# Two-part attention kernel: normalising the second part's sums by a ScalarE copy and a GpSimd product

## Chip, cores and metric

The kernel runs on one core of one Trainium2 chip. Times are device microseconds of one execution. The engines are named as the profile has them: PE is TensorE (PEld its weight loads), DVE is VectorE, ACT is ScalarE, POOL is GpSimd, SP issues the DMAs.

## What is computed

The input is x, of shape (8, 512, 128). The first part adds a causal attention with 16 heads of width 8, whose weights come from four Newton steps. The second part applies six layers, each with a local attention (16 heads of width 64, windows of 32 positions that also see the window before) and a feed-forward block. The place that is changed belongs to the local attention. Cut to that:

```
for i in range(6):
    x = attn_layer(shift_tokens(x), Wqkv[i], q_scale[i], k_scale[i], Wo[i]) + x
    x = ffn_layer(shift_tokens(x), ln_g[i], ln_b[i], W1[i], b1[i], W2[i], b2[i]) + x

# in attn_layer, after l2 norm and rotary embedding of q and k
sim  = einsum('bhwie,bhwje->bhwij', bq, bk2) * 8.0      # 32 queries, 64 keys a window
attn = softmax(where(mask, -max, sim), -1)
out  = einsum('bhwij,bhwje->bhwie', attn, bv2)          # the sums of v
return out.reshape(...) @ Wo
```

The softmax's division is done last: exponentials are not normalised, v carries a column of ones, and the sums of v are divided by the sum that this column gives.

## The kernel before

The first part is a generator (`stieltjes`) that is advanced a few steps at a time by the second part's loop. It runs alone at first, then beside the second part, and is used up about 3600 us into the span; from there on the second part runs alone.

The second part goes through 48 units (a sequence and a layer). A unit has eight pairs of heads, and a pair is one turn of the main loop, so there are 384 turns. Quarters of a unit hold two pairs. One turn does work for several pairs at once:

- `turn` transposes the queries and keys of the newest pair (L629, PE) and copies them out of PSUM (L634, ACT, tiles qT);
- `gather` takes the pair that is three turns older: 64 small matmuls (L683) put its sums of v, and the sums of the exponentials, into a PSUM tile named po2 (po in the profile, which leaves numbers out); L691 takes the reciprocals and L692 the product, both on DVE, into the SBUF tile o2;
- `turn_weights` transposes the exponentials of the pair between (L672) and copies them out (L673, ACT, tile prT);
- `prepare_qk` projects q and k for a later quarter: L563 (PE, tile m), square on ACT (L569), sums of squares on DVE (L572), product with the rotary tables on DVE (L573), sum of halves on POOL (L580), then L586 on DVE, L587 and L588 on ACT for the norms, and the product with them on POOL (L591);
- `exponentials` runs L665 on ACT;
- `turn_sums` transposes o2 (L700, PE) and copies it out (L704, ACT);
- `weigh` computes the scores (L648, PE), adds the band (L653, DVE), takes the maximum (L658, DVE) and subtracts it (L659, POOL);
- `prepare_v` projects v (L600, PE; L603, ACT), and `spread` sends it through DMA into its layout by windows;
- `leave` multiplies by the output weights (L708, PE). A unit ends with an add to xT, and a feed-forward block (L729 to L781) is spread over the turns that follow.

The PSUM tile of the scores and that of the sums of v share one buffer: tag "two" in a pool with one buffer of two banks. L648 can therefore start only when the sums have left it.

The order of instructions on each engine is made when the kernel is built, by a scheduler that works from the program's dependences; on the chip each engine takes its own queue in order. Only a few places are held by hand, through `follow` on ACT. An instruction that waits therefore holds all that is queued behind it on its engine.

Of the kernel before, what the change touches and what calls it, by code (L numbers as in the profile page):

```python
# [12 lines left out]
ALU = mybir.AluOpType  # L13
# [3 lines left out]
P = 128  # L17
N = 512
NT = N // P
# [10 lines left out]
DHL = 64  # L30
# [20 lines left out]
def tile_kernel(  # L51
# [18 lines left out]
    nc = tc.nc  # L70
# [604 lines left out]
    def gather(a):  # L675
        g, p, prT = a["g"], a["p"], a["prT"]
        po = ps_b.tile([P, 2, N], F32, name="po2", tag="two")
        po = po[:, :, 0 : NT * (DHL + 1)].rearrange("p e (c f) -> p e c f", c=NT)
        for n in range(NQ):
            c, u = n // UB, n % UB  # L680
            for e in range(2):
                rows = slice(e * KB, (e + 1) * KB)
                nc.tensor.matmul(  # L683
                    po[u * QB : (u + 1) * QB, e, c, :],
                    lhsT=prT[rows, c, u * QB : (u + 1) * QB],
                    rhs=g["v3"][rows, n, p, :],
                    start=True, stop=True,
                )
        a["o"] = o = tp.tile([P, NT, 2, DHL], F32, name="o2", bufs=2)
        rs = tp.tile([P, 2, NT], F32, name="rs", bufs=2)  # L690
        nc.vector.reciprocal(rs, po[:, :, :, DHL])  # L691
        nc.vector.tensor_tensor(  # L692
            o.rearrange("p c e f -> p e c f"), po[:, :, :, 0:DHL],
            rs.unsqueeze(3).to_broadcast([P, 2, NT, DHL]), ALU.mult,
        )

    def turn_sums(a):
# [136 lines left out]
    while t < slots + LAG + 1 or parts:  # L834
        i, p = t // PQ, t % PQ
# [10 lines left out]
        if last:  # L846
            gather(last)
# [103 lines left out]
```

## Time and profile before

| | |
|---|---|
| median of 3 runs | 5065.17 us (5059.89 to 5066.66) |
| the profiled execution | 5068.51 us, span 5066.8 us |
| mean granted TensorE clock | 0.932 |
| busy | PE 83%, DVE 82%, ACT 69%, POOL 59% |
| L691 (reciprocals), DVE | 384 instructions, 198 ns each |
| L692 (product), DVE | 384 instructions, 685 ns each |

The profile is one execution; shares are of its span. A group's line gives the source line, engine and operation, what is written and read, the count, the busy time and the mean of one, and then the idle time of the engine just before these instructions with what ended most of it. In the lines by stretch the columns are the stretch, its length, then busy time and count of PE, PEld, DVE, ACT and POOL, the granted clock, the DMA share and GB/s. In a timeline the columns are start, length, engine, line, operation, and in brackets the idle time before.

### The profile page before, as it was taken

The numbers are of one execution on the slowest core, as the hardware profiler recorded it, in microseconds if no ns is written. First come the engines' busy times: TensorE is split into PE (matmuls) and PEld (weight loads), VectorE is DVE, ScalarE is ACT, GpSimd is POOL, SyncE is SP. The second block draws the span as 40 slices with busy tenths as digits, with TensorE's granted clock in tenths as the row PEclk, the third lists the DMA queues.
The fourth block names the chain that finished last, engine by engine and source line by source line (L and its number), as shares of the span: only waits on it lengthen the run. The fifth ranks groups of instructions, "written<-read, shape, count | busy, mean of one in ns | idle before, by whom it ended". The sixth has DMA issues, their size and how long they took to land. (4 is left out here: it accounts for less than half of the span.)

```text
span 5066.8 us, 166956 instructions
## 1 busy us (share of the span) xinstructions
PE 4207.6 (83%) x68749; PEld 2541.9 (50%) x68749; DVE 4134.0 (82%) x9460; ACT 3515.5 (69%) x6298; POOL 2980.1 (59%) x3821
## 2 busy tenths in 40 slices
PE   4556598888888887798888888888999999989998
PEld 1223254555555554455555555455655555555554
DVE  6678688988888998888898999888777777777775
ACT  6777677777777777767777877778555555555554
POOL 3345366656666565665666666566566666666663
PEclk6667699999999998899999999999999999999999
DMA  2000022222222221222222222122333232332322
GB/s 66 1 24 18 11 65 51 58 69 51 62 55 64 63 53 35 53 64 53 57 53 63 49 52 63 42 63 56 83 73 75 67 82 66 75 78 68 81 65 54
DMA packets 558921, 288.95 MB, mean 57 GB/s; under 512 B 97580, under 2 KB 541264, under 8 KB 558160
## 3 DMA queue, kind: packets, MB, share of 16 engines
q1 hardware_dynamic: 558160, 278.26, 22.8%
q8 instruction: 543, 8.90, 0.8%
q14 instruction: 218, 1.79, 0.1%
HBM read 66.21 MB, written 7.34 MB: 15 GB/s over the span
## 5 line engine op out<-in xcount | busy, mean ns | idle before, releaser
L580 POOL TENSOR_TENSOR qn<-qr 128x512 f32<-128x512 f32 x768 | 978.0, 1278 | 1374.5 <-DVE qr L573 920.9
L573 DVE TENSOR_TENSOR qr<-m,tab 128x1024 f32<-128x1024 f32 x768 | 928.1, 1216 | 29.3 <-POOL qn L591 1.7
L563 PE MATMUL m<-wqkv,xs 128*128 128x512 f32 x1536 | 772.1, 619 | 63.6 <-ACT qT L634 42.5
L591 POOL TENSOR_TENSOR qn<-qn,ss 128x512 f32<-128x512 f32 x768 | 785.7, 1045 | 59.6 <-ACT ss L588 57.7
L572 DVE TENSOR_REDUCE ss<-qr 128x8 f32<-128x512 f32 x768 | 515.4, 677 | 291.5 <-ACT qr L569 290.1
L281 ACT ACTIVATE d<-ns,lam 128x416 f32<-128x416 f32 (+7 forms) x1024 | 574.3, 623 | 197.1 <-DVE lam L299 159.9
L634 ACT COPY qT<-ptq 128x512 f32<-128x512 f32 x768 | 424.7, 583 | 312.4 <-PE ptq L629 311.2
L264 POOL TENSOR_TENSOR df<-ns,lam 128x160 f32<-128x160 f32 (+7 forms) x1024 | 398.8, 427 | 393.2 <-DVE lam L299 337.3
L569 ACT ACTIVATE qr<-m 128x512 f32<-128x512 f32 x768 | 455.3, 599 | 208.4 <-PE m L563 203.2
L284 DVE BATCH_NORM_STATS2 stw<-d 128x6 f32<-128x416 f32 (+7 forms) x1024 | 518.3, 561 | 96.8 <-ACT d L282 95.7
L600 PE MATMUL pv<-wqkv,xs 128*128 128x256 f32 x1536 | 447.9, 414 | 166.2 <-ACT oT L704 105.1
L629 PEld LDWEIGHTS ptq<-ident,qn 128*128 128x128 f32 x3072 | 362.7, 143 | 243.7 <-issue 136.0
L629 PE MATMUL ptq<-ident,qn 128*128 128x128 f32 x3072 | 444.7, 280 | 32.3 <-DVE qr L573 18.1
L603 ACT COPY v<-pv 128x512 f32<-128x512 f32 x384 | 225.1, 586 | 310.9 <-PE pv L600 193.1
L252 PE MATMUL s<-kn,qj 32*32 32x416 f32 (+15 forms) x4096 | 375.0, 446 | 72.7 <-DVE mn L256 62.3
L659 POOL TENSOR_TENSOR pr<-pr,nm 128x512 f32<-128x512 f32 x384 | 401.2, 1045 | 40.7 <-DVE nm L658 36.0
L316 PE MATMUL dTp<-ident,ns 128*128 128x128 f32 x1280 | 253.6, 310 | 189.9 <-POOL ns L264 84.3
L708 PE MATMUL acc<-oT,wo 128*128 128x512 f32 x768 | 398.8, 601 | 3.8 <-ACT oT L704 3.8
L683 PE MATMUL po<-v,prT 64*32 64x65 f32 x24576 | 391.9, 226 | 11.7 <-DVE pr L653 9.7
L563 PEld LDWEIGHTS m<-wqkv,xs 128*128 128x128 f32 x1536 | 264.5, 196 | 260.4 <-issue 133.8
L600 PEld LDWEIGHTS pv<-wqkv,xs 128*128 128x128 f32 x1536 | 266.3, 194 | 254.2 <-ACT oT L704 149.0
L282 ACT ACTIVATE d<-d 128x1856 f32<-128x1856 f32 (+1 forms) x256 | 392.4, 1533 | 0.0
(135 smaller groups left out, 8139.0 us busy)
## 6 DMA issues: line engine op xcount, KB each, us to landing
v<-v SPq DMA_DIRECT2D x2304, 65.0 KB
v<-v SPq DMA_DIRECT2D x768, 48.8 KB
wqkv<-in_L_ffn_Wqkv_dram SPq DMA_DIRECT2D x72, 256.0 KB
v<-v SPq DMA_DIRECT2D x384, 32.5 KB
wqkv<-in_L_ffn_Wqkv_dram SPq DMA_DIRECT2D x72, 128.0 KB
wo<-in_L_ffn_Wo_dram SPq DMA_DIRECT2D x36, 256.0 KB
tab<-tabs SPq DMA_DIRECT2D x36, 256.0 KB
w<-in_L_ffn_W_dram SPq DMA_DIRECT2D x18, 341.0 KB
```

Source lines behind the costliest of these rows:

```text
L281: nc.scalar.activation(o, n, AF.Ln, bias=lam[:, c : c + 1])
L284: nc.vector.bn_stats(t["st"][:, 4 * rb + a].rearrange("p u k -> p (u k)"), o)
L563: nc.tensor.matmul(m.rearrange("p t h e -> p t (h e)"), lhsT=xs[:, c * P : (c + 1) * P], rhs=wqkv[:, 0:2, q0 : q0 + HQ * DHL], start=True, ...
L569: marks["act"] = nc.scalar.activation(sq, m.rearrange("p t h e -> p (t h) e"), AF.Square)
L572: nc.vector.tensor_reduce(ss[:, i, :], sq, axis=AX.X, op=ALU.add)
L573: nc.vector.tensor_tensor(qr, m.unsqueeze(1).to_broadcast([P, 2, 2, HQ, DHL]), tab[:, i].rearrange("p (k t) e -> p k t e", k=2).unsqueeze( ...
L580: nc.gpsimd.tensor_tensor(g["qn"][:, c].rearrange("p t h (u e) -> p (t h) u e", u=2), halves_of[:, 0], halves_of[:, 1, :, ::-1, :], ALU.add,)
L591: nc.gpsimd.tensor_tensor(qc, qc, ss[:, i, :].unsqueeze(2).to_broadcast([P, 2 * HQ, DHL]), ALU.mult)
L600: nc.tensor.matmul(pv[:, i], lhsT=xs[:, c * P : (c + 1) * P], rhs=cols, start=True, stop=True,)
L629: nc.tensor.transpose(pt[:, c * P : (c + 1) * P], g["qn"][:, c, t, 2 * p : 2 * p + 2, :].rearrange("p h e -> p (h e)"), ident,)
L634: nc.scalar.copy(q, pt)
L659: nc.gpsimd.tensor_tensor(flat, flat, nm.unsqueeze(2).to_broadcast([P, 2 * NT, KB]), ALU.add)
```

## The change

After the gather, the sums of v are copied from PSUM to o2 by ScalarE as they are; VectorE takes the reciprocals; GpSimd multiplies o2 by them in place. One line more stands in the file, so later lines count one up: the copy is L692, the reciprocals L693, the product L694, and the transposes of `turn_sums` L701.

```
         a["o"] = o = tp.tile([P, NT, 2, DHL], F32, name="o2", bufs=2)
         rs = tp.tile([P, 2, NT], F32, name="rs", bufs=2)
+        oe = o.rearrange("p c e f -> p e c f")
+        nc.scalar.copy(oe, po[:, :, :, 0:DHL])
         nc.vector.reciprocal(rs, po[:, :, :, DHL])
-        nc.vector.tensor_tensor(
-            o.rearrange("p c e f -> p e c f"), po[:, :, :, 0:DHL],
-            rs.unsqueeze(3).to_broadcast([P, 2, NT, DHL]), ALU.mult,
+        nc.gpsimd.tensor_tensor(
+            oe, oe, rs.unsqueeze(3).to_broadcast([P, 2, NT, DHL]), ALU.mult,
         )
```

The built program's order is made anew with these instructions, on all engines.

## The prediction

> **What bounds the kernel now.** I read the page first, then the groups, then busy time by stretch, then the timeline of one turn of the main loop. The page shows five engines of which none is busy throughout; the two GpSimd rows are the price list for the new multiply, a 128x512 product with one broadcast operand.
>
> ```profile
> span 5066.8 us, 166956 instructions
> PE 4207.6 (83%) x68749; PEld 2541.9 (50%) x68749; DVE 4134.0 (82%) x9460; ACT 3515.5 (69%) x6298; POOL 2980.1 (59%) x3821
> L591 POOL TENSOR_TENSOR qn<-qn,ss 128x512 f32<-128x512 f32 x768 | 785.7, 1045 | 59.6 <-ACT ss L588 57.7
> L659 POOL TENSOR_TENSOR pr<-pr,nm 128x512 f32<-128x512 f32 x384 | 401.2, 1045 | 40.7 <-DVE nm L658 36.0
> ```
>
> The groups give what goes away (L692), what a ScalarE copy out of PSUM costs (L673), and who waits for the old product (L700).
>
> ```profile
> L692 DVE TENSOR_TENSOR o<-po,rs 128x512 f32<-128x512 f32 x384 | 262.9, 685 | 7.0
> L700 PE MATMUL po<-ident,o 128*128 128x128 f32 x1536 | 243.0, 280 | 98.8 <-DVE o L692 62.9 <-ACT prT L673 16.7 <-DVE sw L294 6.9
> L673 ACT COPY prT<-pT 128x512 f32<-128x512 f32 x384 | 225.1, 586 | 184.6 <-PE pT L672 184.0
> ```
>
> The stretches show that the average over the span hides two regimes: from 600 to 3500 us both parts run together and VectorE is the busiest; from 3600 us the second part runs alone and TensorE is, at 91%, with VectorE at 74%.
>
> ```profile
> 600.00:3500.00 2900.00, 2483.95 (x40055) 1479.52 (x40048) 2558.24 (x6084) 2195.47 (x3898) 1790.49 (x2368) 0.95 0.23 56
> 3600.00:5000.00 1400.00, 1272.10 (x23423) 822.71 (x23417) 1033.72 (x1726) 808.80 (x1624) 870.97 (x853) 1.00 0.31 74
> ```
>
> L691 runs once per turn of the loop, and the same view filtered by L691 counts 216 turns in the first stretch (13.43 us a turn) and 155 from 3600 us on. The timeline of one late turn has the whole question in it: what GpSimd is doing while the sums wait to be transposed.
>
> ```profile
> 4265.31 1.28 POOL L580 TENSOR_TENSOR qn<-qr 128x512 f32<-128x512 f32 x1 [1.04 <-DVE ss L586]
> ...
> 4265.90 0.96 PE L683 MATMUL po<-v,prT 64*32 64x65 f32 x64
> ...
> 4266.54 2.05 POOL L591 TENSOR_TENSOR qn<-qn,ss 128x512 f32<-128x512 f32 x2
> ...
> 4266.90 0.21 DVE L691 RECIPROCAL rs<-po 128x8 f32<-128x8 f32 x1 [1.07 <-PE po L683]
> 4267.15 0.69 DVE L692 TENSOR_TENSOR o<-po,rs 128x512 f32<-128x512 f32 x1
> ...
> 4267.28 1.88 PE L563 MATMUL m<-wqkv,xs 128*128 128x512 f32 x4
> 4267.48 0.59 ACT L673 COPY prT<-pT 128x512 f32<-128x512 f32 x1 [0.79 <-PE pT L672]
> ...
> 4268.54 1.05 POOL L659 TENSOR_TENSOR pr<-pr,nm 128x512 f32<-128x512 f32 x1
> ```
>
> L700 follows at 4269.00 without a wait: L672 and L563 on TensorE cover the 0.9 us that VectorE needs. TensorE runs from one instruction to the next, so here the product costs nothing.
>
> **Part by part.** *Taken from VectorE:* 384 x 0.685 = 263 us. After 3600 us this frees nothing: VectorE next waits 1.20 us for the square (L569), which comes from L563. In the middle it takes VectorE from 2558/216 = 11.84 us a turn to 11.15, below TensorE's 2484/216 = 11.50.
>
> *Put on ScalarE:* 384 copies at 0.586 = 225 us. The order of the built program puts the copy between the last qT copy (L634) and prT (L673). ScalarE waits there anyway: 0.79 us in the turn shown, 184.0 us over 182 turns. The copy would run from 4266.90 to 4267.49, just where prT starts. I put it at nothing on the late path; without that cover it delays prT by up to 0.59 us, and prT is wanted a turn later. In the middle ScalarE goes from 10.16 to 10.75 us a turn, still not the busiest. The PSUM pair of banks is released by the copy's end, 0.35 us before the old product's, long before L648 needs it.
>
> *Put on GpSimd:* 384 products, nearest rows L591 and L659 (one operand broadcast over 64, 1045 ns); the upper end is L580 (1278 ns, two full operands). I take 1.045.
>
> *The new wait.* L694 stands in GpSimd's queue behind whatever is there. In the built order, of the last 114 turns 109 have both L591s and L659 ahead of it and the next L580 behind; TensorE still issues L701 right after L672 and the two L563, as before. So in the turn shown: GpSimd is free at 4269.59, L694 ends at 4270.63, L701 starts 0.14 later (the delay between L692 and L700 where TensorE does wait, at 4252.36 and 4252.50): 4270.77 against 4269.00. TensorE stands for 1.8 us, and L648, L600, the output product and the next turn's L563 queue behind it; ScalarE's oT (L704) and the v copy wait for those.
>
> Does GpSimd's chain shift along? It starts from L563 of the turn before, ahead of that turn's stall in TensorE's queue, so most of a first stall doesn't push the next; only L648's result, through L653 ahead of the second L573 on VectorE, does, and L653 has 1.2 us of slack (scores end 4262.15, L653 starts 4263.35). One unit, eight turns from 3700 us, has these shortfalls if nothing else moved (GpSimd free + 1.04 + 0.14, less the start of L700): 1.87, 2.49, 0.35, 1.98, 1.87, and three below zero, where feed-forward matmuls lengthen the turn. With each stall carried on, and the chain late by the larger of the shift two turns back and the last shift less 1.2: 1.9, then 2.49 + 0.67 - 1.87 = 1.3, 0, 2.0, 0.7, 0, 0, 0. Sum 5.8 us a unit. 152 turns from 3623 us are 19 units: **+110 us**. Lower end, by the loop that cannot be escaped (L700 to L648 to L653 to L573 to L580, two L591, L659, L694, L701: 1.44 + 0.60 + 1.36 + 1.23 + 2.0 + 1.0 + 1.04 + 0.14 = 8.8 us against turns of 8.28, 8.01, 8.05, 8.14 and 8.52): 3.0 a unit, +58. With 1278 ns for L694 the same steps give 6.7 a unit, +128.
>
> The Trainium skill speaks against this change in "GPSIMD Engine Reference", section "Engine selection": elementwise work on two inputs belongs on VectorE, and GpSimd takes about twice as long. The rows here say 1045 against 685, a factor of 1.5; by the rule's two, L694 would take 1.37 us and the late stretch would cost some 136 us, an estimate from that page.
>
> *The middle.* Gain: if the turn follows its busiest engine, from VectorE's 11.84 to TensorE's 11.50, 13.43 x 0.34/11.84 = 0.39 a turn, 83 us; at most the whole 0.69, 149 us. Loss: L694 behind GpSimd's queue, the shortfall worked out as above, is 0.87 a turn on average, 188 us if all of it stood. But TensorE idles 13.43 - 11.50 = 1.9 us a turn and its order is looser. I pass on a third, 63 us, nearer to little than to all: L700 waited there for L692 29.7 us in all, though VectorE was the fullest. Net **-20**, between -149 and +188.
>
> *The shared memory side.* Rows first: L742, a VectorE tensor_scalar on 128x128, took 1.13 us at 4249.63 beside a GpSimd L591 that ended at 4250.68, and 0.30 each at 4252.28 with GpSimd idle; L586 averages 253 ns against a median of 165. GpSimd's share rises by 401/5067 = 8 points, and 384 x 0.088 us of L586's excess at 59% makes 34 us, so 5 us more: **+5**.
>
> "GPSIMD Engine Reference", section "Key points", says more: GpSimd shares its SBUF interfaces with VectorE, and contends also with VectorE instructions that have two SBUF inputs. It gives no price, and no row here isolates such an instruction.
>
> **The sum.** 5068.5 (the profiled execution, span 5066.8 and 1.7 around it) + 110 - 20 + 5 = 5163.5. The median of the runs lies 3.3 below the profiled one: 5160.
>
> **The rivals.** *The middle pays for the late stretch (faster), 0.09.* VectorE is the fullest there at 88%; if the whole 0.685 x 216 = 149 us comes through and the late stretch costs its lower 58, the time is 5065 - 91 = 4974. It decides once the middle gains more than 110/216 = 0.51 us a turn. Against it: TensorE, at 11.50 us, is hardly less full, and waits more.
>
> *The late wait is covered (slightly faster), 0.06.* If L591 and L659 came earlier than the trace has them, only the middle's -20 is left: 5045. Against it: their inputs come from L573 and L588, which follow L563 of the same turn.
>
> *The middle stalls too, 0.09.* If the 0.87 a turn is passed on in full and VectorE's relief is lost, 5065 + 110 + 188 = 5363. For it: in the middle L264 stands in GpSimd's queue in runs of 8 or 16, and a run of 16 took 9.78 us at 3018.98, waiting on lam; 20 turns of the built order have 8 of them just ahead of L694. Against it: TensorE's idle time.
>
> **How the numbers follow.** The forecast has 0.76. Its own bounds, lower late cost with the balanced middle gain and upper late cost with a lost gain, are 5065 + 58 - 83 = 5040 and 5065 + 128 + 63 = 5256; I give 5040 to 5255, which leaves out the first and third rivals, 0.18 in all. A measurement of this kernel tells about 0.2% (10 us) from no change. Faster 0.13 (0.09 from the first rival, 0.04 from the second), same 0.05 (0.02 from the second, 0.03 from the forecast's low end), slower 0.82 (0.73 from the forecast, 0.09 from the third rival).
>
> **What would show it.** Right: from 3600 us on, TensorE idle before L701 with L694 as releaser, about 5.8 us a unit, units of 81 us instead of 75; GpSimd busy from L580 to L694 without a gap; VectorE's share down by 5 points; L694 near 1045 ns; ScalarE's wait before prT shorter by about the copy. The middle should be within some tens of us of its length. Wrong: L701 starting without a wait in late turns (the cover holds), L694 far from 1.0 us, or a middle that gets shorter by more than 110 us.

## The result, and the profile after

The changed kernel takes 5329.47 us (median of 4 runs, 5320.59 to 5335.71) against 5065.91 us before (4 runs, 5059.89 to 5071.55): a ratio of 1.0519, 95% interval 1.0498 to 1.054. It is slower, by 263.6 us; forecast were 95 us, and the range ended at 5255. One execution of the experiments below (dve_product_rf, 7832 us beside 5151 to 5164) was in a slower state and is left out of its median. The profiled execution took 5320.59 us, at a mean granted clock of 0.915 (before: 0.932).

The page after, the two lines that answer to those shown first in the prediction:

```profile
span 5318.9 us, 167209 instructions
PE 4296.5 (81%) x68749; PEld 2583.3 (49%) x68749; DVE 3967.9 (75%) x9076; ACT 3729.3 (70%) x6682; POOL 3371.4 (63%) x4205
```

VectorE is relieved, and TensorE, with exactly the same 68749 matmuls, is busy for 89 us more than before: its matmuls have become longer on average. The groups after, with the new product (L694), the transposes (L701), prT (L673), the new copy (L692) and the reciprocals (L693):

```profile
L694 POOL TENSOR_TENSOR o<-o,rs 128x512 f32<-128x512 f32 x384 | 400.3, 1043 | 316.7 <-DVE rs L693 260.4 <-DVE sw L294 28.5 <-DVE lam L299 9.6
...
L701 PE MATMUL po<-ident,o 128*128 128x128 f32 x1536 | 273.1, 303 | 382.0 <-POOL o L694 374.8 <-ACT prT L673 3.6 <-ACT pr L665 1.8
...
L673 ACT COPY prT<-pT 128x512 f32<-128x512 f32 x384 | 227.6, 593 | 19.0 <-PE pT L672 18.3
L692 ACT COPY o<-po 128x512 f32<-128x512 f32 x384 | 225.5, 587 | 77.4 <-PE po L683 76.5 <-issue 0.2
...
L693 DVE RECIPROCAL rs<-po 128x8 f32<-128x8 f32 x384 | 76.7, 200 | 325.1 <-ACT o L692 324.7
```

Before, TensorE stood 98.8 us ahead of the transposes; now 382.0, nearly all for L694. The product's own length is what the neighbouring rows said (1043 ns). And VectorE's reciprocals, which read only PSUM, wait 324.7 us for ScalarE's copy of the same tile.

To compare the same work, I cut each profile at the starts of the reciprocals, one to a turn, 384 in all:

| us | to turn 16 | turns 16 to 232 (both parts) | turns 232 to 383 (second part alone) |
|---|---|---|---|
| before | 787 | 2844 | 1406 |
| after | 807 | 2953 | 1529 |
| difference | +20 | +109 | +123 |

What is behind the last turn is 30 us in both. Busy time by stretch, cut at turns 16, 232, 240 and 376, so that before and after hold the same work (the second line is 17 units of the late stretch). Before:

```profile
787.20:3631.07 2843.87, 2449.68 (x39687) 1462.21 (x39687) 2501.07 (x5888) 2138.62 (x3802) 1753.00 (x2295) 0.96 0.24 56
3706.31:4985.16 1278.85, 1160.57 (x21400) 750.11 (x21399) 941.09 (x1567) 736.99 (x1480) 797.72 (x780) 1.00 0.31 73
```

After:

```profile
806.99:3760.15 2953.16, 2482.67 (x39672) 1483.26 (x39672) 2425.49 (x5668) 2244.18 (x4010) 1972.75 (x2510) 0.94 0.23 54
3841.47:5227.11 1385.64, 1211.16 (x21399) 770.06 (x21398) 858.27 (x1430) 821.36 (x1617) 934.40 (x916) 0.96 0.29 67
```

Late, a unit went from 1278.85/17 = 75.2 us to 81.5. Of these 6.3 us, TensorE's idle time is 3.3 (118.28 to 174.48 over 17 units) and its busy time 3.0 (1160.57 to 1211.16), with the granted clock down from 1.00 to 0.96. In the middle the 109 us are 76 of idle time and 33 of longer matmuls.

The timeline of one late turn after the change, with other rows left out, shows the wait as the prediction had it: copy, reciprocals, and then GpSimd's queue.

```profile
4199.76 1.27 POOL L580 TENSOR_TENSOR qn<-qr 128x512 f32<-128x512 f32 x1 [1.32 <-DVE ss L586]
...
4200.99 2.04 POOL L591 TENSOR_TENSOR qn<-qn,ss 128x512 f32<-128x512 f32 x2
...
4201.74 0.58 ACT L692 COPY o<-po 128x512 f32<-128x512 f32 x1 [0.20 <-PE po L683]
...
4202.35 0.21 DVE L693 RECIPROCAL rs<-po 128x8 f32<-128x8 f32 x1 [2.07 <-ACT o L692]
...
4202.99 1.04 POOL L659 TENSOR_TENSOR pr<-pr,nm 128x512 f32<-128x512 f32 x1
...
4203.99 1.04 POOL L694 TENSOR_TENSOR o<-o,rs 128x512 f32<-128x512 f32 x1
...
4205.08 0.66 PE L701 MATMUL po<-ident,o 128*128 128x128 f32 x4 [1.12 <-POOL o L694]
```

Copy and reciprocals are done at 4202.56; GpSimd needs until 4205.03, because L591 twice and L659 are ahead. The turn before started its L701 at 4196.19, 8.89 us earlier.

What the prediction had no term for is seen on TensorE's own timeline (TensorE alone) around one longer wait of the late stretch:

```profile
4412.37 1.12 PE L701 MATMUL po<-ident,o 128*128 128x128 f32 x4 [2.86 <-POOL o L694]
4413.41 1.18 PE L648 MATMUL s<-qT,qT 64*32 64x64 f32 x64
4414.53 2.07 PE L600 MATMUL pv<-wqkv,xs 128*128 128x256 f32 x4
4416.39 1.91 PE L709 MATMUL acc<-oT,wo 128*128 128x512 f32 x2
...
4423.51 0.66 PE L701 MATMUL po<-ident,o 128*128 128x128 f32 x4 [0.67 <-POOL o L694]
4424.10 0.86 PE L648 MATMUL s<-qT,qT 64*32 64x64 f32 x64
4424.89 1.13 PE L600 MATMUL pv<-wqkv,xs 128*128 128x256 f32 x4
```

The same L701 takes 1.12 us after a wait of 2.86 and 0.66 after one of 0.67; L648 1.18 against 0.86, L600 2.07 against 1.13. The stretches over this place give the granted clock (the third column from the right):

```profile
4412.40:4414.50 2.10, 2.10 (x68) 1.63 (x68) 0.00 (x0) 0.58 (x1) 1.14 (x1) 0.50 0.09 22
4414.50:4416.50 2.00, 2.00 (x11) 1.62 (x6) 1.86 (x4) 0.00 (x0) 0.00 (x0) 0.50 0.00 0
4416.50:4420.00 3.50, 3.50 (x46) 1.94 (x45) 0.63 (x2) 1.02 (x3) 2.27 (x2) 0.70 0.00 0
```

TensorE stands 2.86 us, and then runs at half clock for some 6 us: the mean of 0.70 in the last stretch is half clock up to about 4418.6 and full clock after it. Such a wait (2.8 to 3.0 us) comes once in most late units, for instance at 4330.64, 4412.37 and 4494.48, 82 us apart.

In the middle the wait is longer and rarer. One turn from the timeline of all engines:

```profile
2038.34 0.58 ACT L692 COPY o<-po 128x512 f32<-128x512 f32 x1 [1.61 <-PE po L683]
...
2043.68 7.58 POOL L264 TENSOR_TENSOR ns<-ns,lam 128x416 f32<-128x416 f32 x10 [1.62 <-DVE lam L299]
...
2047.51 0.20 DVE L693 RECIPROCAL rs<-po 128x8 f32<-128x8 f32 x1
...
2051.22 3.10 POOL L264 TENSOR_TENSOR df<-ns,lam 128x160 f32<-128x160 f32 x8
...
2054.28 2.23 POOL L264 TENSOR_TENSOR ns<-ns,lam 128x224 f32<-128x224 f32 x6
...
2056.47 1.04 POOL L694 TENSOR_TENSOR o<-o,rs 128x512 f32<-128x512 f32 x1
...
2057.57 1.11 PE L701 MATMUL po<-ident,o 128*128 128x128 f32 x4 [8.95 <-POOL o L694]
```

The reciprocals wait in VectorE's queue, 8.59 us beyond the copy's end at 2038.92, and are done at 2047.71. Then the first part's 24 L264 stand ahead of L694 in GpSimd's queue, so it runs 8.76 us later, and TensorE stands 8.95 us. Over the whole middle, TensorE's waits after the change:

```profile
PE po L701 <- POOL o L694: 199.8, 126, 8.9
```

(Total us, times, longest.) Before, the same stretch (600 to 3600 us) had 31.1 us of waits of L700 for L692.

How much later the sums are ready can be read turn by turn from the traces. From the last matmul of a gather (L683) to the end of the instruction that the transposes wait for, mean us a turn:

| | turns 16 to 232 | turns 232 to 383 |
|---|---|---|
| before | 3.22 | 1.37 |
| after | 5.32 | 3.45 |
| of what is added: the copy | 0.59 | 0.59 |
| the reciprocals' wait after the copy | 1.01 | 0.26 |
| the product's wait after the reciprocals, in VectorE's queue before and GpSimd's after | 0.16 (0.63 to 0.79) | 1.00 (0.15 to 1.15) |
| the longer product | 0.36 | 0.35 |

The rest is the wait ahead of the first of these instructions, which hardly changed. So late it is mostly GpSimd's queue; in the middle the new step on ScalarE, and VectorE's queue behind it, are the larger part.

### The profile page after: what moved, and what is told of

Read it like the earlier page. It is cut to its first block, busy times and chain, and to the rows that moved or that the text cites. A ratio compares the mean times of both kernels' runs of the same rounds, so it can differ in the third digit from the quotient of the medians.

```text
span 5318.9 us, 167209 instructions
## 1 busy us (share of the span) xinstructions
PE 4296.5 (81%) x68749; PEld 2583.3 (49%) x68749; DVE 3967.9 (75%) x9076; ACT 3729.3 (70%) x6682; POOL 3371.4 (63%) x4205
## 5 line engine op out<-in xcount | busy, mean ns | idle before, releaser
L573 DVE TENSOR_TENSOR qr<-m,tab 128x1024 f32<-128x1024 f32 x768 | 928.2, 1217 | 30.1 <-DVE ss L572 2.2
L591 POOL TENSOR_TENSOR qn<-qn,ss 128x512 f32<-128x512 f32 x768 | 784.9, 1043 | 126.9 <-ACT ss L588 125.0
L264 POOL TENSOR_TENSOR df<-ns,lam 128x160 f32<-128x160 f32 (+7 forms) x1024 | 398.4, 425 | 335.9 <-DVE lam L299 259.4
L694 POOL TENSOR_TENSOR o<-o,rs 128x512 f32<-128x512 f32 x384 | 400.3, 1043 | 316.7 <-DVE rs L693 260.4
L701 PE MATMUL po<-ident,o 128*128 128x128 f32 x1536 | 273.1, 303 | 382.0 <-POOL o L694 374.8
L600 PE MATMUL pv<-wqkv,xs 128*128 128x256 f32 x1536 | 478.9, 437 | 60.2 <-DVE qr L573 30.8
L701 PEld LDWEIGHTS po<-ident,o 128*128 128x128 f32 x1536 | 182.4, 151 | 596.2 <-POOL o L694 557.4
L659 POOL TENSOR_TENSOR pr<-pr,nm 128x512 f32<-128x512 f32 x384 | 400.3, 1043 | 53.5 <-DVE nm L658 48.7
L709 PE MATMUL acc<-oT,wo 128*128 128x512 f32 x768 | 418.6, 628 | 0.8 <-ACT oT L705 0.8
L648 PE MATMUL s<-qT,qT 64*32 64x64 f32 x24576 | 384.7, 235 | 41.6 <-DVE rs L693 39.7
L252 PE MATMUL s<-kn,qj 32*32 32x416 f32 (+15 forms) x4096 | 361.7, 434 | 55.8 <-DVE mn L256 45.0
```

Of the source, the lines that this page charges most:

```text
L573: nc.vector.tensor_tensor(qr, m.unsqueeze(1).to_broadcast([P, 2, 2, HQ, DHL]), tab[:, i].rearrange("p (k t) e -> p k t e", k=2).unsqueeze( ...
L591: nc.gpsimd.tensor_tensor(qc, qc, ss[:, i, :].unsqueeze(2).to_broadcast([P, 2 * HQ, DHL]), ALU.mult)
L600: nc.tensor.matmul(pv[:, i], lhsT=xs[:, c * P : (c + 1) * P], rhs=cols, start=True, stop=True,)
L694: nc.gpsimd.tensor_tensor(oe, oe, rs.unsqueeze(3).to_broadcast([P, 2, NT, DHL]), ALU.mult,)
L701: nc.tensor.transpose(pt[:, c * P : (c + 1) * P], a["o"][:, c].rearrange("p e f -> p (e f)"), ident)
L709: nc.tensor.matmul(acc, lhsT=wo[:, pp % (NPAIR // 2), :], rhs=a["oT"], start=(pp == 0), stop=(pp == NPAIR - 1),)
```

## Experiments

Theory Queue: the place of the product in GpSimd's queue is the cost, in both stretches. Rivals: ScalarE's copy (its time, or the reciprocals that wait for it); and in the middle VectorE's relief, whatever it is worth. All medians are of runs beside runs of the kernel before on the same chip (5060 to 5068 us); the splits by turns are from each run's profile. Later kernels build on the order with the reciprocals first, which the first experiment brought.

**recip_first**: the reciprocals ahead of the copy.

```
-        nc.scalar.copy(oe, po[:, :, :, 0:DHL])
         nc.vector.reciprocal(rs, po[:, :, :, DHL])
+        nc.scalar.copy(oe, po[:, :, :, 0:DHL])
```

> The change with its reciprocals ahead of its copy, so that ScalarE's copy waits for 0.2 us of VectorE and not VectorE for ScalarE's queue. Two theories for the 135 us or so that the middle stretch (turns 10 to 232) lost against the kernel before. Queue: TensorE stands for the product in GpSimd's queue; then little changes, 5300 to 5340 us. Reciprocal wait: VectorE stands in its own order for the copy, and all behind it is late; then the middle's loss goes, 5150 to 5220 us, and the late stretch keeps its 118 us.

Measured 5310.62 (ratio 1.0478, 1.046 to 1.0495): 19 us below the change. Nothing is gained from two reads in parallel, since they still go one after the other: now the copy waits for the reciprocals.

```profile
L701 PE MATMUL po<-ident,o 128*128 128x128 f32 x1536 | 268.6, 300 | 359.9 <-POOL o L694 351.9 <-ACT prT L673 3.2 <-ACT qr L569 2.0
...
L693 ACT COPY o<-po 128x512 f32<-128x512 f32 x384 | 225.5, 587 | 151.9 <-DVE rs L692 145.6 <-DVE mv L172 1.2 <-DVE lam L268 1.2
```

TensorE's wait for L694 is 351.9 us against 374.8. The wait between copy and reciprocals is real, but the exchange only turns it round: in the middle the copy now stands 1.22 us a turn behind the reciprocals (the reciprocals stood 1.01 behind the copy), and the sums are ready after 5.32 us as before the exchange.

**dve_product**: the copy stays on ScalarE, the product goes back to VectorE.

```
-        nc.gpsimd.tensor_tensor(
+        nc.vector.tensor_tensor(
             oe, oe, rs.unsqueeze(3).to_broadcast([P, 2, NT, DHL]), ALU.mult,
```

> The change with its product on VectorE (in place on the copied sums), so GpSimd has no part in it; copy and reciprocals stay as they are. Queue: all of the loss goes, 5040 to 5100 us. Reciprocal wait: the late stretch's 118 us go, the middle's 135 stay, 5170 to 5230 us.

Measured 5168.24 (1.0203, 1.0188 to 1.0218), late 1433, middle 2912: between the two theories. 161 of the 264 us go away with GpSimd's product; the detour through ScalarE has a price of its own, which I had not expected. In the middle the sums are still ready 1.87 us a turn later than before the change (5.09 against 3.22), with GpSimd out of the chain. Part of it is the product itself:

```profile
L694 DVE TENSOR_TENSOR o<-o,rs 128x512 f32<-128x512 f32 x384 | 349.4, 910 | 6.1
```

910 ns against 685 when its input was in PSUM (the last section has why).

**dve_copy**: the copy on VectorE, the product on GpSimd; VectorE is not relieved and ScalarE not loaded.

```
-        nc.scalar.copy(oe, po[:, :, :, 0:DHL])
+        nc.vector.tensor_copy(oe, po[:, :, :, 0:DHL])
```

> The change with its copy out of PSUM on VectorE, not ScalarE: the product stays on GpSimd, but nothing waits for ScalarE, and VectorE is not relieved (a copy of 128x512 for a product of 128x512). Queue: as slow as the change or slower by what VectorE's relief was worth, 5320 to 5420 us. Reciprocal wait: the middle's loss goes, about 5185 us.

Measured 5327.3 (1.0514, 1.0498 to 1.0529), as slow as the change; the middle is 2963 us against 2953. So taking 0.685 us a turn from VectorE and giving 0.587 to ScalarE is worth 10 us in the middle, not the 83 of the forecast. That is its worth with the wait for GpSimd standing in both kernels; turn_later, below, asks the same with the wait covered. The sums are ready after 5.01 us in the middle: the reciprocals' wait falls from 1.01 to 0.33, and the product's in GpSimd's queue rises from 0.79 to 1.19.

```profile
L701 PE MATMUL po<-ident,o 128*128 128x128 f32 x1536 | 268.5, 300 | 374.9 <-POOL o L694 371.0 <-ACT prT L673 2.1 <-POOL df L264 1.5
...
L692 DVE COPY o<-po 128x512 f32<-128x512 f32 x384 | 262.0, 682 | 220.6 <-PE po L683 220.2
```

**mid_only**: the change in the first 28 units alone, that is up to turn 224.

```
+        if g["u"] < 28:
             (copy, reciprocals, GpSimd product)
+        else:
+            (reciprocals, VectorE product from PSUM)
```

> The change for units 0 to 27 only (pairs 0 to 223, while the first part still runs); units 28 to 47 as in the kernel before. Both theories: 5180 to 5225 us, the middle's loss alone, with L693 and L701 waiting there as in the change. If it came near 5066, the middle's loss would be an effect of the late stretch's order and both theories would be wrong about the place.

Measured 5199.58 (1.0261, 1.0246 to 1.0276), within the expectation: middle 2964, late 1401. The two costs stand side by side and add up; the middle is a loss by itself.

**dve_extra**: the kernel before, with one more VectorE instruction a turn off the path (its output is not used).

```
+        nx = tp.tile([P, 2 * NT], F32, name="nx")
+        nc.vector.tensor_reduce(nx, o.rearrange("p c e f -> p (c e) f"), axis=AX.X, op=ALU.max)
```

> The kernel before with one more VectorE reduction over the normalised sums per turn, 128x512 as L658 (674 ns); nobody reads its result. It prices 0.67 us of VectorE a turn, the amount that the change takes off. If the middle is bound by how full VectorE is (the prediction's step, 0.39 to 0.69 us a turn), it costs 83 to 150 us: 5150 to 5215. If the middle is bound by waits that run from engine to engine through the queues, VectorE's share is worth little either way: 5070 to 5110.

Measured 5116.63 (1.0103, 1.0085 to 1.0121), between the two expectations. The instruction takes 678 ns, 146 us over the middle, and costs 59 there (2903 against 2844): 40% of its time. VectorE's time does count in the middle, but by less than half. Late, the time is 15 us below before's; the order of the instructions was made anew, and no run isolates why.

**pool_touch**: the kernel before, with an in-place GpSimd copy of 8 elements a partition between product and transposes. It puts a step in GpSimd's queue between product and transposes, and has nothing else of the change.

```
+        nc.gpsimd.tensor_copy(o[:, :, :, 0:1], o[:, :, :, 0:1])
```

> The kernel before with a GpSimd copy of 8 elements a partition, in place, between the product on VectorE and its transposes: GpSimd's queue is on the path with next to no work, ScalarE and VectorE do what they did before. Queue: the late stretch pays the prediction's steps with 0.1 us in place of 1.04, 0.9 + 0.6 + 0 + 1.0 + 0 = 2.5 us a unit, 48 us, and the middle some 40 to 80: 5150 to 5200. If the work on GpSimd and ScalarE is what costs: under 5090.

Measured 5233.2 (1.0333, 1.0317 to 1.035): +171, of it 91 in the middle and 63 late. That is above the expected 5150 to 5200, and above both of its parts (48 us late, 40 to 80 in the middle).

```profile
L701 PE MATMUL po<-ident,o 128*128 128x128 f32 x1536 | 263.4, 296 | 251.5 <-POOL o L696 242.3 <-ACT d L281 5.7 <-ACT qr L569 1.6
...
L696 POOL COPY o<-o 128x8 f32<-128x8 f32 x384 | 77.2, 201 | 278.5 <-DVE o L692 247.4 <-DVE sw L294 11.7 <-DVE stw L292 3.4
```

An instruction of 201 ns, 77 us in all, costs 171: it is the place in the queue that is paid for, not the work. Where GpSimd is free it starts as little as 0.06 us after the product. On average in the middle it starts 1.19 us after; of these 257 us in all GpSimd spends 157 in L264 and 55 in L591. TensorE's waits for it in turns 16 to 232 are (total us, times, longest)

```profile
PE po L701 <- POOL o L696: 128.1, 71, 11.2
```

where the same turns had 29.8 us for the product before: 98 us more, of which 91 come through in the stretch's length. So a place in GpSimd's queue is enough to lose about as much in the middle as the change does, without relief, ScalarE copy or GpSimd product. It doesn't say that the change loses its 109 us by that alone: there the queue holds the product for 0.79 us a turn, and ScalarE's step and VectorE's queue come on top.

**sums_later** and **sums_later_old**: the transposes of the sums later within the turn, behind `prepare_v`, so that TensorE has other work while GpSimd multiplies; once with the change (reciprocals first), once with the old product as a control.

```
-        if last:
-            turn_sums(last)
         (weigh, prepare_v)
+        if last:
+            turn_sums(last)
```

> The change with reciprocals ahead of the copy, and with the transposes of the sums (L701) emitted after the scores and the projection of v, which puts 0.86 and 1.13 us of TensorE's work more between gather and L701. Queue: the wait before L701 is covered in the late stretch (118 us back) and mostly in the middle (60 to 130 back): 5070 to 5150 us. If VectorE's relief is real behind that wait, below 5060. If the work on GpSimd or ScalarE costs by itself, it stays above 5200.

> The control for the last: the kernel before with L700 moved to the same place, product on VectorE. In the kernel before L700 hardly waited (99 us in all), so 5030 to 5090 us by both theories; the difference to the last run is then the price or gain of the change with its wait covered.

Measured 5194.39 (1.0262, 1.0243 to 1.028) and 5099.92 (1.007, 1.0051 to 1.0089). Both miss. The cover works: TensorE's wait for L694 falls to 69.6 us. But the place is a bad one, since the transposes there wait for L573 of VectorE (111.5 and 85.2 us), and the late stretch takes 1481 and 1437. Change against control is +94 us, where it is +243 without the later place (recip_first), so most of the wait's price goes, and not all of it.

**norms_follow** and **norms_later_old**: the two L591 of a turn are put behind the product in GpSimd's queue; the control issues them as late, with the old product and no order by hand.

```
+        owed.append((g, ss, cs))          # end of prepare_qk, in place of the loop
+    def norms():                          # called right after gather(last)
+        for i, c in enumerate(cs):
+            follow(nc.gpsimd.tensor_tensor(qc, qc, ...), marks.get("o"))   # the product
```

> The change, reciprocals ahead of the copy, with both L591 of a turn put behind the next turn's L694 in GpSimd's queue (they are wanted a turn later still). In the late stretch GpSimd is then free 2.0 us earlier, ahead of the copy's end, and L694 ends 0.1 to 0.2 us before TensorE wants it. Queue, by place: the late stretch falls back to 1406 us or near (a gain of 118 on the change) and the middle loses most of the 91 us that the place in the queue costs: 5080 to 5150 us. If the length of the product or the copy were what costs in the late stretch: above 5200.

> The control for the last: the kernel before, with L591 emitted a turn later and product on VectorE, no order forced. L591 is on nobody's path there: 5040 to 5090 us.

Measured 5140.29 (1.0156, 1.014 to 1.0172) and 5059.23 (0.9995, 0.9985 to 1.0004). With L591 gone from ahead of the product, the late stretch takes 1402 us, less than before the change (1406), at a granted clock of 1.00; the late loss is L591's place, as forecast. The middle is 2903, 42 us below recip_first's and still 59 above before's. There L264 still stands ahead of the product (74 of the 100 us between the copies' ends and the products' starts), but that is 0.47 us a turn; the sums are ready after 5.00 us, 1.78 later than before the change, most of it by the copy (0.59), its wait for ScalarE's queue (1.21) and the product, 0.36 longer. The middle's waits of this kernel (its product is L701, its transposes L708):

```profile
PE po L708 <- POOL o L701: 142.9, 130, 6.7
```

**dve_product_rf**: dve_product with the reciprocals first.

> The copy on ScalarE and the product on VectorE as in an earlier run (5168 us), with the reciprocals ahead of the copy, so that VectorE doesn't wait for ScalarE before them; the product still does. If the reciprocals' wait is what cost 100 us there: 5070 to 5110. If the detour over ScalarE's queue costs whichever instruction waits for it, or ScalarE's work itself: 5140 to 5175.

Measured 5156.98 (median of three; 1.0189, 1.0172 to 1.0206), which can't be told from dve_product's 1.0203 and is what the second expectation had; middle 2900, late 1430. VectorE's wait for ScalarE has moved from the reciprocals (256.4 us there) to the product (152.6 here). So it doesn't matter which of the two stands for the copy; the detour through ScalarE's queue, and the work on it, are not told apart.

**act_extra**: the kernel before, with a ScalarE copy of 296 elements a turn off the path (not used).

```
+        ax = tp.tile([P, 296], BF16, name="ax")
+        nc.scalar.copy(ax, o.rearrange("p c e f -> p (c e f)")[:, 0:296])
```

> The kernel before with one more ScalarE copy a turn that nobody reads: 296 of the 512 elements, to a narrow tile, some 0.43 us where the change's copy takes 0.585. It prices ScalarE's time alone, off every path: if ScalarE's fullness costs in the middle like VectorE's (59 us for 0.67 us a turn), 30 to 50 us, 5095 to 5120; if the cost of the copy is its place on the path, under 5085.

Measured 5085.83 (1.0048, 1.0032 to 1.0065), between the expectations. 441 ns a turn, 95 us over the middle, cost 17 there and 3 late. It isn't quite off every path: the copy stands in ScalarE's queue for the product that it reads (104.0 us in all), so the 17 us hold that too.

**turn_later** and **turn_later_old**: a whole turn between gather and transposes, with the change (reciprocals first) and with the old product. Both also take the feed-forward steps of the first two sequences eight a turn in place of four.

```
-    while t < slots + LAG + 1 or parts:
+    while t < slots + LAG + 2 or parts:
+        if LAG + 2 <= t < len(pairs) + LAG + 2:
+            late = pairs[t - LAG - 2]
-        if last:
-            turn_sums(last)
+        if late:
+            turn_sums(late)               # leave and the end of a unit likewise take late
-            many = 4
+            many = 8                      # feed-forward steps a turn, first two sequences
```

> The change, reciprocals ahead of the copy, with the transposes of the sums and the output product a whole turn after the gather, so that nothing is wanted from L694 for some 8 to 13 us; the feed-forward steps of the first two sequences run eight a turn in place of four. If the wait before L701 is all of the loss, the change is now a gain by VectorE's relief: the control less 20 to 60 us in the middle, and equal to the control in the late stretch. If ScalarE's and GpSimd's work or the PSUM tile's release costs by itself, it is 40 to 60 us slower than the control in the middle.

> The control: the kernel before with the same delay of a turn, product on VectorE. L700 hardly waited before, so 5040 to 5110 us; the first turns change by the denser feed-forward steps, in both runs alike.

Measured 5109.18 (1.0094, 1.0077 to 1.0111) and 5090.93 (1.006, 1.0045 to 1.0075). With a turn of slack the change costs 18 us over its control (middle +12, late +11) instead of 243: TensorE's wait for the sums is nearly the whole loss, whichever queue makes them late. The group of transposes in turn_later no longer names L694:

```profile
L701 PE MATMUL po<-ident,o 128*128 128x128 f32 x1536 | 240.9, 279 | 54.5 <-ACT prT L673 53.3 <-POOL pr L659 0.5
```

But no gain shows even so, though 263 us of product are gone from VectorE: the middle is neither 20 to 60 us below the control nor 40 to 60 above. The turn of slack, with the denser feed-forward steps, costs 55 us in the middle with the old product, 40 of it in turns 16 to 96 (1105 us against 1065), and gives 35 late. The two parts of that edit weren't run apart in the middle.

**late_delay_old**: the old product, with the extra turn of slack from unit 28 on only.

```
+            if late["g"]["u"] < 28:
+                late = None
+        if last and last["g"]["u"] < 28:
+            late = last
```

> The kernel before, with transposes of the sums and output product a whole turn after the gather from unit 28 on only, where the second part runs alone; the product stays on VectorE. The middle as before; the late stretch 1371 to 1380 us in place of 1406: 5030 to 5045 us. If the control's gain there came from something set up earlier in the run, 5060 to 5075.

Measured 5035.48 (median of 5, 0.9945, 0.9932 to 0.9959): faster than the kernel before by 29 us, and the only one of these that beats both kernels. The late stretch takes 1367 us. TensorE's waits for L692 ahead of L700 there, 25.9 us before, are gone.

## Why the prediction was wrong, step by step

**The step that failed is the middle: −20 forecast, +109 measured (+129 with the first 16 turns, which had no term).** It had two terms, and both were wrong in the same direction.

*The gain, 83 us "if the turn follows its busiest engine".* dve_copy puts the relief, net of ScalarE's copy, at 10 us, and turn_later shows none with the wait covered. Three readings stand behind that. A turn doesn't follow VectorE: what dve_extra added to it cost 40%. ScalarE's copy wasn't free: at act_extra's rate, 17 us for 95, 0.587 us over 216 turns would cost some 23 (an estimate). And VectorE's busy time over the middle fell by 75.6 us, where 216 x 0.685 = 148 were taken away. Of the 72 us that are missing, 45 are other instructions that got longer: L296 by 9.9 us, L240 by 7.8 (from 801 to 973 ns each over the run), L298 by 6.1 and smaller ones. The other 27 never were there to gain: rows of VectorE overlap a little in time, and with the product its overlaps go too. dve_copy, which has GpSimd's product and as many VectorE instructions as before, has 23.6 us more busy time in the middle; so GpSimd's use is a part of the lengthening, and the rest isn't isolated.

*The loss, "I pass on a third" of 0.87 a turn.* The 0.87 came out near in size: TensorE's waits for the product went from 31.1 to 199.8 us between 600 and 3600 us, 0.79 for each of the 214 turns. But the prediction made it of GpSimd's queue alone; by the traces more of the delay is the copy and VectorE's queue behind it. The third was a guess, and too low: of the waits that pool_touch added in the middle, 91 of 98 us came through, and of those of the change (29.8 to 194.7 us, turns 16 to 232) 109 of 165. Idle time on TensorE was taken for slack. It isn't: it is made of waits for other engines, which wait for TensorE in turn. ScalarE's waits for the transposes (L704 for L700, then L705 for L701) went from 42.8 to 116.5 us in the same turns. A part also comes back as slower matmuls, 33 of the 109 us.

**The rival "the middle stalls too" is nearest to what happened.** It gave 5363 for a full pass-on without relief; the measured 5329 is far closer to it than to 5160. Its mechanism, L264 in runs ahead of the product, is in the trace (8.95 us at 2057.57), but as a part: in the middle the products start 171 us in all after their reciprocals, 76 of it while GpSimd is in L264, 47 in L591 and 20 in L659. It was put at 0.09 on the argument of TensorE's idle time. (The run of 16 at 3018.98 that it cites wasn't waiting on lam: the trace has 16 products there one after the other, without idle time.)

**The late stretch: right in sum, not in its parts.** Forecast were +110, 5.8 us a unit and units of 81 us; measured +123, 6.3 and 81.5; the loop was put at 8.8 us, and the turn shown, a short one, takes 8.89. L694 ends where the queue was worked out to let it end, and norms_follow, which takes L591 from ahead of it, brings 1402 us. But the prediction's 5.8 us were all idle time. Measured are 3.3 of idle time and 3.0 of matmuls at a lower clock, for which it had no term; that the two errors nearly cancel was luck.

**Copy and reciprocals as parallel: wrong, and not small in the middle.** The prediction released the PSUM tile 0.35 us earlier, let both read it at once, and priced the copy by how full ScalarE is. L693 waits 324.7 us for L692, and as one more step between gather and transposes copy and wait take 1.60 us a turn in the middle. The order the other way round saves 19 us in all; dve_product, which keeps the step without GpSimd, still loses 68 us in the middle.

**Other steps.** L694 at 1.045 us: 1.043. ScalarE's wait ahead of prT: from 184.6 to 19.0 us over the span, and from 69.4 to 0.3 late, so the copy fell into it as forecast. "The late wait is covered" (5045) is refuted by 166.2 us of waits for L694 from 3600 us on, "the middle pays" (4974) by a middle that is 109 us longer. The shared memory side, +5, was probably put too small: VectorE's longer instructions took back 45 of 148 us of busy time in the middle, and dve_copy has 23.6 with GpSimd's product alone.

**What stays open.** Why the change nets nothing (+18) when its wait is covered. ScalarE's copy would explain it by the rate above; GpSimd's product off the path wasn't priced by itself. How the middle's 109 us divide between ScalarE's step, VectorE's queue and GpSimd's queue is known as delay (0.59, 1.01 and 0.79 us a turn), not as time of the kernel: the runs that take one away change another with it (dve_copy). And a remade order can move a stretch by some 15 us with no cause that I could name (dve_extra's late stretch is 15 below before's), so terms below that can't be told apart here.

## What to carry to other kernels

Price an operation that moves to another engine by what stands ahead of it in that engine's queue and by who waits for its result, turn by turn, before counting what the old engine saves: here 201 ns of GpSimd work a turn cost 171 us. Count every engine that is put in between, each with its own queue. In this loop, whose engines are 60 to 90% busy and wait for one another, idle time wasn't slack, and the relief of the fullest engine came through in small part or not at all. If the consumer can be moved later by a turn where that is cheap, most of such a wait goes; ask that of the kernel as it stands too, where it gave 0.55%.

## What the runs showed of the hardware

**After a wait of nearly 3 us TensorE mostly runs at half clock.** Over the changed kernel from 600 us on, the four transposes L701 took 0.60 to 0.70 us as a rule. Of 324 that followed a wait under 2.6 us or none, 17 took over 0.9; of 44 after a longer one, 31 did, up to 1.12 (of the 16 after 2.8 to 3.0 us, 15). Before the change only 4 of 371 had such a wait. The Trainium skill, "TensorE: Matmul & The Clock Gate", section "HAM oscillation — how this bites in real kernels", wants no idle gap of TensorE above some 3.4 us. Here waits of 2.8 to 3.0 us did it once in most late units. A stall's price is then its length and some 2.5 us more: L701, L648, L600 and L709 took 6.28 us in the turn shown, and 3.76 in the turn before it (0.66, 0.95, 1.13 and 1.02, by the timeline).

**A VectorE product with both inputs in SBUF is held up by GpSimd.** In dve_product L694 on VectorE took 681 ns on average when GpSimd was idle at its start (207 times) and 1177 when it was busy (177 times). One took 6.23 us; the timeline of that place in dve_product:

```profile
2957.34 1.29 POOL L580 TENSOR_TENSOR qn<-qr 128x512 f32<-128x512 f32 x1
...
2957.94 6.23 DVE L694 TENSOR_TENSOR o<-o,rs 128x512 f32<-128x512 f32 x1
...
2958.59 1.04 POOL L659 TENSOR_TENSOR pr<-pr,nm 128x512 f32<-128x512 f32 x1
...
2959.59 0.91 POOL L264 TENSOR_TENSOR df<-ns,lam 128x160 f32<-128x160 f32 x2
...
2960.46 2.04 POOL L591 TENSOR_TENSOR qn<-qn,ss 128x512 f32<-128x512 f32 x2
...
2962.46 2.72 POOL L264 TENSOR_TENSOR df<-ns,lam 128x224 f32<-128x224 f32 x6
```

GpSimd works back to back the whole time. This agrees with the contention that the Trainium skill, "GPSIMD Engine Reference", section "Key points", states for VectorE instructions with two SBUF inputs. The prediction found no row for it; the kernel before has a small one, L270 (mn and lam, 128x16): 163 ns on average with GpSimd idle at its start, 549 with it busy. The old product took one input from PSUM, and 681 ns with GpSimd idle at its start against 687 with it busy. The Trainium skill, "SBUF — State Buffer", section "SBUF: two separate sides", has the later of the two blocked until the other's instruction ends. The 6.23 us here outlast several GpSimd instructions, none over 1.29 us.

**Two engines' reads of one PSUM tile went one after the other.** Copy and reciprocals only read po. Yet L693 waited for L692 (324.7 us in 178 waits), and with the lines exchanged the copy waited for the reciprocals (145.6 us). In no one of the 384 turns of either kernel do the two overlap. The waits are for semaphores, so it is the program's order, and no run here tells what the memory itself would do.
